# A four-layer Flamingo kernel: the 16-head attentions of layers 1 and 3 as pipelines of 16 tiles, their masks as matrix products

## The chip, the core and the metric

The kernel runs on one core of one Trainium2 chip. The metric is device time in microseconds of one execution, from launch to end. Three timed executions of the kernel before are at hand, and one execution taken by the hardware profiler. Engines are named as the profile names them: PE is TensorE (matrix products), PEld its weight loads, DVE is VectorE, ACT is ScalarE, POOL is GpSimd, SP is SyncE, which here only issues transfers.

## The reference, cut to what matters

A residual stream `x` of 2 x 1024 tokens of width 256 goes through four layers. Each layer adds a gated cross-attention to a context of 64 tokens per batch, and then a gated feed-forward block of eight experts. Only the attentions of layers 1 and 3 change:

```python
# layer 1 (layer 3 is alike, with its own weights)
qh = (q @ Wq.T + bq).reshape(B, Qlen, 16, 16).transpose(0, 2, 1, 3)     # q = layernorm(x)
kh = (k @ Wk.T + bk).reshape(B, Klen, 16, 16).transpose(0, 2, 1, 3)     # k = v = context
vh = (v @ Wv.T + bv).reshape(B, Klen, 16, 16).transpose(0, 2, 1, 3)
score = jnp.einsum('bhqd,bhkd->bhqk', qh, kh) / 4
score = jnp.where(kv_mask[:, None, None, :], score, -10000.0)           # layer 1: per key
# layer 3:  scores = jnp.where(m == 0, -1e9, scores), m per query and key
attn = jax.nn.softmax(score, axis=-1)
out = jnp.einsum('bhqk,bhkd->bhqd', attn, vh).transpose(0, 2, 1, 3).reshape(B, Qlen, 256)
x = x + tanh(g) * (out @ Wo.T + bo)
```

Layer 1 then adds `tanh(g) * sum_e (silu(h @ Wg[e]) * (h @ Wu[e])) @ Wd[e]` with `h = layernorm(x)`, over all eight experts for every token. Layer 3 routes each token to its two best experts, with a capacity of 320 places for each expert. Layer 2 has an attention of a single shared head and a routed feed-forward block.

## The kernel before

All arithmetic is float32, apart from small bfloat16 products in the routers. The 2048 tokens are 16 tiles of 128 tokens, and four tiles make a group; `xs` holds the whole residual stream in SBUF. A float32 matrix product stands in the trace as two MATMUL records.

The class `Heads` (L411) is the attention of 16 heads. `query_steps` makes the transposed queries of a group (L493, L494) and adds the output bias to `xs` on POOL (L501). Then four steps follow for each tile:

- `scores` (L503): four products of 64 rows by 256 columns (L515) put the scores of 8 heads into each of two PSUM banks. In layer 1, DVE adds the key mask (L532), finds the maxima (L547) and subtracts them (L548), and one ACT instruction takes the exponentials of all 1,024 columns (L555). In layer 3, DVE writes -1e9 over masked scores with a predicated copy (L526) and finds the negated maxima (L540); then ACT takes the exponentials of one head at a time, 16 instructions of 64 columns, with the maximum as the bias (L543).
- `turned` (L562): eight PE transposes (L571) and two ACT copies out of PSUM (L177).
- `quotients` (L579): 16 narrow products for the sums and 16 for the values (L590). In layer 1, two DVE reciprocals (L610) and one multiplication (L611) follow. In layer 3, which sets `by_log`, ACT takes a logarithm and an exponential (L602, L603) and DVE does three operations (L604 to L606).
- `output` (L614): two products with the output weights (L264), and DVE adds the result to `xs` (L621).

`norm_steps` (L230) is a layer norm of a group: statistics on DVE, the normed rows `h`, then eight transposes (L256). `h` is made by DVE (L246), or by ACT where `by_act` is set (L241).

In layer 1, `middle` (L1744) calls `first` for each group: norm, attention, the norm for the feed-forward block, and four DVE operations that prepare Strassen operands (`rhs_blocks`). Group 0 runs under pools that own all eight PSUM banks. The other three groups share two PSUM banks (`Both`) with the feed-forward block: `first(1)` is written ahead of `ffn1_group(0)`, `first(2)` behind it, and `first(3)` behind `ffn1_group(1)`. The block of a group is 672 products of 128 x 256 (L1644 and L1689; 1,344 records), in a Strassen-like scheme; POOL forms the sums of weights (L1275 to L1278). Behind each block but the last stands `last(g)`, the single-head attention of layer 2. What is written one after the other does not run so: the recording layer puts the instructions of each engine in an order of its own, as far as data and buffers allow, and so mixes the attention of a group among the products of the block before it.

In layer 3, `last_attention` (L1828) already runs the 16 tiles as one pipeline: for each step it calls `turned` of the tile before, `scores`, `quotients` of the tile before and `output` of the one before that, and puts in between them steps of the norm and queries of the group to come (`ready`) and of the norm and routing of the group that is done (`onward`).

Of the kernel before, what the change touches and what calls it, by code (L numbers as in the profile page):

```python
# [8 lines left out]
F32 = mybir.dt.float32  # L9
# [9 lines left out]
P = 128  # L19
# [11 lines left out]
EPS = 1e-5  # L31
NEG = -1.0e9

L0_W = 128
# [9 lines left out]
def kernel(ctx: ExitStack, tc: tile.TileContext, a: dict, out: bass.AP):  # L44
# [51 lines left out]
    def small_copy(src, name):  # L96
# [3 lines left out]

    ramp_b, upper_b, ones_b = (
        small_copy(t, n) for t, n in ((ramp, "ramp_b"), (upper, "upper_b"), (ones, "ones_b"))
    )
# [125 lines left out]

    def norm_steps(g, psp, hpool, hTpool=None, by_act=False):  # L230

        xg = xs[:, g * TG : (g + 1) * TG, :]
        mv, rstd = stats(xg, TG, by_act)
        yield
        h = hpool.tile([P, TG, D], F32, name="h")
        if by_act:
            off = small.tile([P, TG], F32, name="off")
            V.scalar_tensor_tensor(off, mv[:, :, 0], -1.0, rstd, ALU.mult, ALU.mult)
        for t in range(TG):
            if by_act:  # L240
                A.activation(  # L241
                    h[:, t, :], xg[:, t, :], AF.Identity,
                    bias=off[:, t : t + 1], scale=rstd[:, t : t + 1],
                )
            else:
                V.tensor_scalar(  # L246
                    h[:, t, :], xg[:, t, :], mv[:, t, 0:1], rstd[:, t : t + 1],
                    ALU.subtract, ALU.mult,
                )
            if t % 2:  # L250
                yield
        hT = (hTpool or hpool).tile([P, NC, GW], F32, name="hT")
        for c in range(NC):
            ps = psp.tile([P, GW], F32, name="ps_tr")
            for t in range(TG):
                T.transpose(ps[:, t * P : (t + 1) * P], h[:, t, c * P : (c + 1) * P], ident)  # L256
            evac(1 if by_act else c, hT[:, c, :], ps)
            yield
        return h, hT
# [151 lines left out]
    class Heads:  # L411


        def __init__(self, pre, c_bk, r_bv, r_bo, gate, key_mask, full_mask):
# [3 lines left out]
            self.live, self.qT = {}, {}  # L418

        def setup(self, psp, tag):  # L420

# [10 lines left out]
            if key_mask is not None:  # L432
                km_u = held.tile([P, B * SK // 4], I32, name="km_u")
                nc.scalar.dma_start(
                    km_u, key_mask.rearrange("b k -> (b k)").partition_broadcast(P)
                )
                km = held.tile([P, B * SK], F32, name="km")
                V.tensor_single_scalar(km, km_u.bitcast(U8), 0.0, ALU.not_equal)
                self.kbias = held.tile([P, B * SK], F32, name="kbias")
                V.tensor_scalar(self.kbias, km, -1.0, 10000.0, ALU.add, ALU.mult)  # L440
            if full_mask is not None:
                m_w = wpool.tile([P, 2048], F32, name="w")
                m_i = m_w[:, : NT * SK].rearrange("p (t k) -> p t k", k=SK).bitcast(I32)
                nc.scalar.dma_start(
                    m_i, full_mask.rearrange("b (t p) k -> p (b t) k", p=P)
                )
                self.dropm = held.tile([P, NT, SK], U8, name="dropm")
                V.tensor_single_scalar(self.dropm, m_i, 0.0, ALU.is_equal)
            for c in range(NC):
# [53 lines left out]
        def scores(self, tt, pools):  # L503
# [7 lines left out]

            pair = [pss.tile([P, 512], F32, name="ps_s") for _ in range(2)]
            for c in range(NC):
                for r in range(2):
# [4 lines left out]
                        .rearrange("p j k -> p (j k)"),  # L519
                        start=True, stop=True,  # L520
                    )
            for r in range(2):
                ps3 = pair[r].rearrange("p (j k) -> p j k", k=SK)
                ps4 = pair[r].rearrange("p (c j k) -> p c j k", c=NC, k=SK)
                if self.full_mask is not None:
                    V.copy_predicated(  # L526
                        out=ps3,
                        mask=self.dropm[:, tt, :].unsqueeze(1).to_broadcast([P, HC, SK]),
                        data=negs.unsqueeze(2).to_broadcast([P, HC, SK]),
                    )  # L530
                if self.key_mask is not None:
                    V.tensor_add(  # L532
                        ps3, ps3,
                        self.kbias[:, b * SK : (b + 1) * SK].unsqueeze(1)
                        .to_broadcast([P, HC, SK]),
                    )
                mx = two.tile([P, HC], F32, name="mx")
                if self.full_mask is not None:

# [13 lines left out]
                )  # L553
            if self.full_mask is None:
                A.activation(pr, pr, AF.Exp)  # L555
            self.live[tt] = pr

        def values(self, tt, pools):
            self.turned(tt, pools)
            self.quotients(tt, pools)  # L560

# [60 lines left out]

        def group(self, g, hT, pools):

            self.queries(g, hT, pools)
            for i in range(TG + 2):
                if i < TG:
                    self.scores(g * TG + i, pools)
                if 0 <= i - 1 < TG:
                    self.values(g * TG + i - 1, pools)  # L630
                if 0 <= i - 2:
                    self.output(g * TG + i - 2, pools)

# [1110 lines left out]
    def middle():  # L1744
        with ExitStack() as es:
            two = es.enter_context(tc.tile_pool(reuse_waits="tile", name="mi_two", bufs=2))
            hp = es.enter_context(tc.tile_pool(reuse_waits="tile", name="mi_h", bufs=1))
            hTp = es.enter_context(tc.tile_pool(reuse_waits="tile", name="mi_hT", bufs=1))
            hT1p = es.enter_context(tc.tile_pool(reuse_waits="tile", name="mi_hT1", bufs=2))
            hT1 = {}  # L1750

            def first(g, pools):
                _, hT = norm_group(g, pools["pt"], hp, hTp)
                heads1.group(g, hT, pools)
                _, hT = norm_group(g, pools["pt"], hp, hT1p)
                t = hT1p.tile([P, 4, 256], F32, name="xsum")
                hT1[g] = hT, rhs_blocks(
                    hT[:, 0, :256], hT[:, 0, 256:], hT[:, 1, :256], hT[:, 1, 256:],
                    [t[:, i] for i in range(4)],
                )  # L1760


            with ExitStack() as wide:
                pools = {"two": two}
                for n, bufs in (("pt", 2), ("ps", 4), ("py", 2)):
                    pools[n] = wide.enter_context(
                        tc.tile_pool(reuse_waits="tile", name="mw_" + n, bufs=bufs, space=PSUM)
                    )
                first(0, pools)

            py = es.enter_context(tc.tile_pool(reuse_waits="tile", name="mi_py", bufs=2, space=PSUM))
# [20 lines left out]
            pb = seed_banks(pbp)  # L1792
            first(1, pools)
            for g in range(NG):
                ffn1_group(g, hT1[g], pools, pb)
                if g + 2 < NG:
                    first(g + 2, pools)
                if g + 1 < NG:
                    run(last(g))
# [28 lines left out]
    def last_attention():  # L1828
        with ExitStack() as es:
# [15 lines left out]
            def ready(g):  # L1845
                _, hT = yield from norm_steps(g, pools["pt"], hp, hTp, by_act=True)
                yield from heads3.query_steps(g, hT, pools)

            def onward(g):
                h, hT = yield from norm_steps(g, pools["pt"], hp2, by_act=True)  # L1850
                yield from router3.group_steps(g, h, hT, pr, rp)

            run(ready(0))
            coming, gone = [], []

            def between(n):
                advance(coming)
                advance(gone, n)  # L1860

            for i in range(NT + 2):
                if i < NT and i % TG == 0:
                    advance(coming, 99)
                    if i + TG < NT:
                        coming.append(ready(i // TG + 1))
                if 0 <= i - 1 < NT:
                    heads3.turned(i - 1, pools)
                if i < NT:
                    heads3.scores(i, pools)  # L1870
                between(2)
                if 0 <= i - 1 < NT:
                    heads3.quotients(i - 1, pools)
                between(2)
                if 0 <= i - 2:
                    heads3.output(i - 2, pools)
                if i > TG and i % TG == 1:
                    gone.append(onward(i // TG - 1))
                between(1)
            advance(gone, 99)  # L1880

# [114 lines left out]
```

## Time and profile before

| what | us |
|---|---|
| timed executions | 2265.69, 2277.82, 2279.7 (median 2277.82) |
| profiled execution, its own time | 2266.35 |
| span of its trace, first to last instruction | 2264.3 |
| busy in the span: PE / DVE / ACT / POOL | 2075.5 / 1389.0 / 967.2 / 1105.6 |
| 0 to 346: layer 0 | 346, PE busy 276.3, clock 0.87 |
| 346 to 394: attention of layer 1, group 0 | 48, PE busy 35.3, clock 0.71 |
| 394 to 1682: feed-forward of layer 1, with the attention of groups 1 to 3 and three of the single-head attentions | 1288, PE busy 1272.0, clock 1.00 |
| 1682 to 1930: rest of layer 2 | 248, PE busy 205.9 |
| 1930 to 2101: attention and routing of layer 3 | 171, PE busy 141.1, clock 0.84 |
| 2101 to 2264: feed-forward of layer 3 | 163, PE busy 144.9, clock 0.93 |

The clock is the mean share of TensorE's full speed that was granted in the stretch. Matrix products are pipelined, and the ends that the trace gives them are modelled, so a busy PE is not always a PE at its peak; where it matters, starts are compared with starts.

### The profile page before, as it was taken

How to read it: one execution, taken by the hardware profiler on the slowest of the kernel's cores; microseconds unless marked ns; L12 is line 12 of the kernel's file. 1: busy time of each engine (PE TensorE's matmuls, PEld its weight loads, DVE VectorE, ACT ScalarE, POOL GpSimd, SP SyncE). 2: the span in 40 equal slices, each digit the busy share in tenths (PEclk: the TensorE clock that was granted, in tenths of full speed). 3: DMA queues.
4: the chain of work that ended last, by engine and by line, in shares of the span. 5: the costliest groups of instructions: out<-in, count | busy, mean ns of one | idle time of the engine just before them, and what ended most of it. 6: DMA issues, size and time to landing. Idle time of an engine off the chain costs nothing.

```text
span 2264.3 us, 31677 instructions
## 1 busy us (share of the span) xinstructions
PE 2075.5 (92%) x11232; PEld 1737.0 (77%) x11232; DVE 1389.0 (61%) x3199; ACT 967.2 (43%) x2200; POOL 1105.6 (49%) x1233
## 2 busy tenths in 40 slices
PE   6749997999999999999999999999985998797797
PEld 3439984788888778887788887888864998465797
DVE  5851127876655966566966556665575666576564
ACT  4414431633333533334433333333332654684454
POOL 2226643256665356665366664666631674100674
PEclk8859996999999999999999999999995999797899
DMA  3136442122222122222122222222222444111352
GB/s 101 47 127 192 127 142 85 38 75 92 86 84 75 57 84 84 88 90 70 61 88 90 84 90 78 87 91 85 90 78 72 133 128 104 47 39 57 100 143 63
DMA packets 108533, 201.05 MB, mean 89 GB/s; under 512 B 20052, under 2 KB 47960, under 8 KB 105790
## 3 DMA queue, kind: packets, MB, share of 16 engines
q1 hardware_dynamic: 83144, 162.18, 22.5%
q0 software_dynamic: 19728, 36.03, 6.2%
q8 instruction: 89, 1.46, 0.3%
q10 hardware_dynamic: 5504, 0.82, 0.2%
q14 instruction: 68, 0.56, 0.1%
HBM read 206.89 MB, written 21.91 MB: 101 GB/s over the span
## 4 chain that ended last, share of the span: by engine, by line
PE 76%; DVE 12%; DMA 4%; issue 2%; POOL 2%; ACT 2%; POOLq 0%; SPq 0%; DVEq 0%; ACTq 0%
PE ps_b L1644 14%; PE ps_a L1644 9%; PE ps_e L1644 9%; PE ps_b L1689 6%; PE ps_m L264 6%; PE ps_e L1689 4%; PE ps_a L1689 4%; PE ps_y L934 3%; PE ps_y L264 3%; PE ps_b L1485 2%; PE ps_b L1512 2%; PE ps_a L1485 2%; PE ps_e L1485 1%; PE ps_e L1512 1%; PE ps_a L1512 1%
## 5 line engine op out<-in xcount | busy, mean ns | idle before, releaser
L1644 PE MATMUL ps_b<-xsum,w 128*128 128x256 f32 x1536 | 389.6, 381 | 3.3 <-DVE c L1670 2.7
L1275 POOL TENSOR_TENSOR w<-w 128x256 f32<-128x256 f32 x220 | 162.2, 737 | 449.4 <-DMA w<-in_L_Wu_dram 182.9
L1644 PEld LDWEIGHTS ps_b<-xsum,w 128*128 128x128 f32 x1536 | 288.9, 190 | 51.4 <-issue 7.3
L1326 ACT COPY u<-ps_b 128x512 f32<-128x512 f32 (+5 forms) x242 | 119.2, 493 | 432.3 <-PE ps_b L1689 241.8
L1644 PE MATMUL ps_a<-hT,w 128*128 128x256 f32 x1024 | 266.6, 380 | 0.7 <-DVE hT L179 0.7
L1644 PEld LDWEIGHTS ps_a<-hT,w 128*128 128x128 f32 x1024 | 192.0, 190 | 29.0 <-issue 2.0
L1276 POOL TENSOR_TENSOR w<-w 128x256 f32<-128x256 f32 x220 | 190.0, 864 | 0.0
L1278 POOL TENSOR_TENSOR w<-w 128x256 f32<-128x256 f32 x220 | 181.1, 823 | 16.7
L1277 POOL TENSOR_TENSOR w<-w 128x256 f32<-128x256 f32 x220 | 188.8, 858 | 0.0
L1308 ACT COPY ps_b<-ps_a 128x512 f32<-128x512 f32 (+5 forms) x242 | 116.1, 480 | 129.7 <-DVE b L1674 75.2
L1314 ACT COPY m<-ps_e 128x512 f32<-128x512 f32 (+5 forms) x242 | 118.2, 489 | 41.0 <-PE ps_e L1689 26.7
L1644 PE MATMUL ps_e<-xsum,w 128*128 128x256 f32 x512 | 133.3, 379 | 0.0
L1644 PE MATMUL ps_e<-hT,w 128*128 128x256 f32 x512 | 132.9, 380 | 0.0
L1706 POOL TENSOR_TENSOR m<-m,accT 128x256 f32<-128x256 f32 x60 | 71.2, 1186 | 125.8 <-ACT m L1314 119.7
L1689 PE MATMUL ps_a<-b,w 128*128 128x256 f32 x512 | 132.3, 379 | 0.0
L886 POOL DMA_INDIRECT xg<-hd_L,r_idx x48 | 46.6, 971 | 175.0 <-DVE r_wsl L870 87.3
L1689 PE MATMUL ps_b<-t,w 128*128 128x256 f32 x512 | 130.9, 379 | 0.0
L1670 DVE TENSOR_TENSOR c<-ps_e,u 128x512 f32<-128x512 f32 x64 | 44.2, 691 | 136.8 <-ACT u L1326 136.8
L1671 DVE TENSOR_TENSOR b<-b,c 128x512 f32<-128x512 f32 x128 | 117.4, 917 | 3.9
L1644 PEld LDWEIGHTS ps_e<-hT,w 128*128 128x128 f32 x512 | 96.4, 190 | 14.6 <-issue 1.3
L1689 PEld LDWEIGHTS ps_b<-t,w 128*128 128x128 f32 x512 | 97.0, 190 | 13.7 <-DVE accT L1707 0.5
L1689 PEld LDWEIGHTS ps_a<-b,w 128*128 128x128 f32 x512 | 96.9, 190 | 13.9 <-issue 0.9
(423 smaller groups left out, 4550.1 us busy)
## 6 DMA issues: line engine op xcount, KB each, us to landing
w<-in_L_Wg_dram SPq DMA_DIRECT2D x64, 512.0 KB, 4.0
w<-in_L_Wu_dram SPq DMA_DIRECT2D x64, 512.0 KB, 4.0
w<-in_L_Wd_dram SPq DMA_DIRECT2D x64, 512.0 KB, 3.6
w<-in_L_W_dram SPq DMA_DIRECT2D x64, 512.0 KB, 4.3
hd_L<-h SPq DMA_DIRECT2D x8, 512.0 KB, 2.9
b<-b2d SPq DMA_DIRECT2D x23, 128.0 KB, 3.1
xs<-in_x_dram SPq DMA_DIRECT2D x4, 512.0 KB, 5.5
xd<-xs SPq DMA_DIRECT2D x4, 512.0 KB, 2.8
```

Of the source, the lines that this page charges most:

```text
L264: T.matmul(ps, lhsT=lhs(c), rhs=rhs(c), start=(c == 0), stop=(c == n - 1))
L1275: lambda: eng.tensor_add(s[0], a21, a22),
L1276: lambda: eng.tensor_sub(s[1], s[0], a11),
L1277: lambda: eng.tensor_sub(s[2], a11, a21),
L1278: lambda: eng.tensor_sub(s[3], a12, s[1]),
L1308: A.copy(self.b, self.pa)
L1314: A.copy(self.sb5, self.pe)
L1326: A.copy(u2, self.b)
L1485: T.matmul(ps[:, q * half : (q + 1) * half], lhsT=w[kind][:, q, :], rhs=x[kind], start=(first and q == 0), stop=True, skip_group_check=True,)
L1644: T.matmul(ps[:, q * 256 : (q + 1) * 256], lhsT=lhs[kind][:, q, :], rhs=xr[kind], start=(first and q == 0), stop=True, skip_group_check=True,)
L1671: V.tensor_mul(m[name], m[name], c)
L1689: T.matmul(ps, lhsT=wd[kind][:, q, :], rhs=m["rhs"][kind][:, q * 256 : (q + 1) * 256], start=(clear and q == 0), stop=True, skip_group_che ...
```

## The change

Six edits belong together.

1. **Order.** The loop of `last_attention` becomes the method `Heads.pipeline`, and layer 1 uses it too: all 16 tiles run under the eight-bank pools ahead of the first `ffn1_group`, with three `two` buffers, two query buffers and `by_log`. The normed rows and Strassen sums of all four groups are kept until their blocks (`hT1p` has four buffers instead of two).
2. **Masks.** The predicated copy of layer 3 and the addition of layer 1 go. In their place stands a bfloat16 product of 128 x 512 in front of the scores of each bank, which opens the bank's accumulation; the score products add to it. In layer 3 it is the identity times a mask of 0 and -2^60, in layer 1 a matrix of ones times a row pattern that sums to -10000 for a masked key.
3. **Maxima.** In layer 3 the second bank of each tile is done as in layer 1: DVE subtracts the maxima of 8 heads in one instruction, and ACT takes the exponentials of its 512 columns in one.
4. **Norms.** Where `halved` is set, two of the four rows of tiles of a norm go to POOL.
5. **Quotients.** In layer 1, `by_log` replaces the two reciprocals and the multiplication by the forms of layer 3.
6. **Setup.** `kbias` and `dropm` become bfloat16, with three small DVE operations more.

```diff
-    def norm_steps(g, psp, hpool, hTpool=None, by_act=False):
+    def norm_steps(g, psp, hpool, hTpool=None, by_act=False, halved=False):
...
-            if by_act:
+            if by_act and (t % 2 or not halved):
                 A.activation(
...
+            elif by_act:
+                G.tensor_scalar(
+                    h[:, t, :], xg[:, t, :], rstd[:, t : t + 1], off[:, t : t + 1],
+                    ALU.mult, ALU.add,
                 )
...
+            self.by_head = 0 if full_mask is None else 1
...
-                self.kbias = held.tile([P, B * SK], F32, name="kbias")
-                V.tensor_scalar(self.kbias, km, -1.0, 10000.0, ALU.add, ALU.mult)
+                two_rows = held.tile([P, 2], F32, name="two_rows")
+                V.tensor_scalar(two_rows[:, 0:1], partid, 0.0, 9984.0, ALU.is_equal, ALU.mult)
+                V.tensor_scalar(two_rows[:, 1:2], partid, 1.0, 16.0, ALU.is_equal, ALU.mult)
+                V.tensor_add(two_rows[:, 0:1], two_rows[:, 0:1], two_rows[:, 1:2])
+                self.kbias = held.tile([P, B * SK], BF16, name="kbias")
+                V.tensor_scalar(self.kbias, km, -1.0, two_rows[:, 0:1], ALU.add, ALU.mult)
...
-                self.dropm = held.tile([P, NT, SK], U8, name="dropm")
-                V.tensor_single_scalar(self.dropm, m_i, 0.0, ALU.is_equal)
+                self.dropm = held.tile([P, NT, SK], BF16, name="dropm")
+                V.tensor_scalar(self.dropm, m_i, 0.0, MASKED, ALU.is_equal, ALU.mult)
...
             pair = [pss.tile([P, 512], F32, name="ps_s") for _ in range(2)]
+            if self.full_mask is not None:
+                whose, drop = ident_b, self.dropm[:, tt, :]
+            else:
+                whose, drop = ones_b, self.kbias[:, b * SK : (b + 1) * SK]
+            for r in range(2):
+                T.matmul(
+                    pair[r], lhsT=whose, rhs=drop.unsqueeze(1).to_broadcast([P, HC, SK]),
+                    start=True, stop=False, skip_group_check=True,
+                )
             for c in range(NC):
                 for r in range(2):
                     T.matmul(
...
-                        start=True, stop=True,
+                        start=False, stop=True, skip_group_check=True,
                     )
...
-                if self.full_mask is not None:
-                    V.copy_predicated(
...
-                if self.key_mask is not None:
-                    V.tensor_add(
...
-                if self.full_mask is not None:
+                if r < self.by_head:
                     V.tensor_reduce(mx, ps3, AX.X, ALU.max, negate=True)
...
-            if self.full_mask is None:
+                if self.by_head:
+                    A.activation(prv[:, r], prv[:, r], AF.Exp)
+            if not self.by_head:
                 A.activation(pr, pr, AF.Exp)
...
-        def group(self, g, hT, pools):
-            self.queries(g, hT, pools)
-            for i in range(TG + 2):
...
+        def pipeline(self, pools, ready, onward):
+            run(ready(0))
+            coming, gone = [], []
+            def between(n):
+                advance(coming)
+                advance(gone, n)
+            for i in range(NT + 2):
+                if i < NT and i % TG == 0:
+                    advance(coming, 99)
+                    if i + TG < NT:
+                        coming.append(ready(i // TG + 1))
+                if 0 <= i - 1 < NT:
+                    self.turned(i - 1, pools)
+                if i < NT:
+                    self.scores(i, pools)
+                between(2)
+                if 0 <= i - 1 < NT:
+                    self.quotients(i - 1, pools)
+                between(2)
+                if 0 <= i - 2:
+                    self.output(i - 2, pools)
+                if i > TG and i % TG == 1:
+                    gone.append(onward(i // TG - 1))
+                between(1)
+            advance(gone, 99)
...
     def middle():
         with ExitStack() as es:
+            hT1p = es.enter_context(tc.tile_pool(reuse_waits="tile", name="mi_hT1", bufs=NG))
+            hT1 = {}
+            with ExitStack() as wide:
...
+                pools = {
+                    "two": wpl("two", 3), "nq": 2, "by_log": True,
+                    "pt": wpl("pt", 2, space=PSUM), "ps": wpl("ps", 4, space=PSUM),
+                    "py": wpl("py", 2, space=PSUM),
+                }
+                hp, hTp = wpl("h", 2), wpl("hT", 2)
+                def ready(g):
+                    _, hT = yield from norm_steps(g, pools["pt"], hp, hTp, by_act=True, halved=True)
+                    yield from heads1.query_steps(g, hT, pools)
+                def onward(g):
+                    _, hT = yield from norm_steps(g, pools["pt"], hp, hT1p, by_act=True, halved=True)
+                    t = hT1p.tile([P, 4, 256], F32, name="xsum")
+                    hT1[g] = hT, rhs_blocks(
...
+                heads1.pipeline(pools, ready, onward)
...
-            hT1p = es.enter_context(tc.tile_pool(reuse_waits="tile", name="mi_hT1", bufs=2))
-            def first(g, pools):
-                _, hT = norm_group(g, pools["pt"], hp, hTp)
-                heads1.group(g, hT, pools)
-                _, hT = norm_group(g, pools["pt"], hp, hT1p)
...
-                first(0, pools)
...
-            first(1, pools)
             for g in range(NG):
                 ffn1_group(g, hT1[g], pools, pb)
-                if g + 2 < NG:
-                    first(g + 2, pools)
                 if g + 1 < NG:
                     run(last(g))
```

## The prediction

> **What bounds the kernel now.** I read the page's 40 slices first, then busy times by stretch, then TensorE's timeline, then groups by shape.
>
> The slices (each 56.6 us) show PE and its granted clock:
>
> ```profile
> PE   6749997999999999999999999999985998797797
> ...
> PEclk8859996999999999999999999999995999797899
> ```
>
> Slices 8 to 30, the feed-forward block of layer 1 with three of the four attention groups in it, are PE at full clock. Slice 7 (group 0) and slices 35 to 37 (layer 3) are not. The stretches say what the block costs. Columns: stretch, length, busy time (instructions) of PE, PEld, DVE, ACT, POOL, clock, DMA:
>
> ```profile
> 480.00:715.00 235.00, 235.00 (x1090) 206.53 (x1089) 144.35 (x209) 87.13 (x167) 150.46 (x182) 1.00 0.28 87
> ```
>
> Only feed-forward products run there: 235 us / 1,089 records = 0.2158 us each. The same stretches asked for L1644 and then L1689 alone (length, PE busy, records):
>
> ```profile
> 715.00:779.00 64.00, 34.38 (x138) 1.00 0.17 52
> ...
> 715.00:779.00 64.00, 9.69 (x37) 1.00 0.17 52
> ```
>
> 175 records x 0.2158 = 37.8 us, so the other 26.2 us of these 64 are the attention of group 2. That attention is not hidden: PE is full, and every PE microsecond of it is on the path.
>
> Layer 3 (1930 to 2101) already runs the pipeline that layer 1 is to get:
>
> ```profile
> 1960.00:2050.00 90.00, 86.67 (x752) 54.82 (x754) 70.30 (x225) 77.18 (x282) 2.35 (x1) 1.00 0.09 31
> 2010.00:2030.00 20.00, 17.68 (x138) 11.07 (x138) 19.73 (x66) 17.99 (x61) 2.35 (x1) 1.00 0.14 49
> 2050.00:2076.00 26.00, 20.61 (x172) 14.95 (x163) 17.53 (x73) 13.80 (x47) 0.00 (x0) 0.74 0.06 21
> ```
>
> PE is 96% busy at full clock in its body; ACT (86%) and DVE (78%) fill up only in bursts, as where the routing stands (DVE 99%), and the last tiles run at clock 0.74. A part of PE's busy time there is no work (start, duration, line, records):
>
> ```profile
> 1970.56 0.60 PE L571 MATMUL ps_tr<-ident,pr 128*128 128x128 f32 x4
> 1971.09 0.70 PE L515 MATMUL ps_s<-kblk,qT 64*128 64x256 f32 x2
> 1971.71 0.44 PE L571 MATMUL ps_tr<-ident,pr 128*128 128x128 f32 x2
> 1972.08 0.70 PE L515 MATMUL ps_s<-kblk,qT 64*128 64x256 f32 x2
> ...
> 1980.53 1.13 PE L515 MATMUL ps_s<-kblk,qT 64*128 64x256 f32 x4
> 1981.59 0.66 PE L256 MATMUL ps_tr<-ident,h 128*128 128x128 f32 x4
> ```
>
> Two score records hold PE 0.62 us before the next instruction, four 1.06: 0.22 each and 0.19 for the change-over. Two transposes hold it 0.37 instead of 0.22: 0.15. So each piece into which a tile's scores are cut costs 0.34.
>
> **Layer 1, before.** From the first transposes of group 0 (350.92) to 394.00: 43.1 us. Then, each time the stretch less its records x 0.2158: 394 to 462, 29.6; 462 to 480, 2.2; 715 to 779, 26.2; 779 to 812, 13.8; 1045 to 1108, 26.5; 1108 to 1137, 11.5. Together 152.9. The stretch 1370 to 1405, where a block ends and layer 2's attention runs with no 16-head attention near, costs 9.8; two such parts of the above remain after the change. Share of the 16-head attention: 133.3 us.
>
> **Layer 1, after**, counted on PE.
> - Head: first transposes to the first tile's quotients took 368.17 - 350.92 = 17.2 us. Two mask additions (1.30 us, L532) leave that path; the mask products run while PE waits for the norm. 16.0. Layer 3's first two tiles stand 10 us apart where later ones stand 6.5, its clock still rising: +3.5.
> - Tiles: layer 3's quotients start at 1964.21, 1968.58, 1974.48, 1982.17 and 1990.20: 26.0 us for four tiles with one set of queries and the transposes of two norms, no routing: 6.50 a tile. Two mask products a tile come on top. No bfloat16 product of 512 columns is in the trace. Nearest from below: eight records of 128 x 120 (L1249) start 0.42 us before the next instruction, 0.44 ns a column, so 0.22 us. From above: a float32 record of 512 columns (L264) takes 0.44. I take 0.23, the same type. 6.96 a tile; 15 tiles: 104.4. They hold three sets of queries and norms instead of 3.75: -3.9. 100.5.
> - Tail: the last tile's quotients (1.0); its logarithm, exponential, three multiplications, output, statistics, norm and transposes (0.47 + 0.46 + 1.26 + 1.1 + 0.48 + 0.75 + 0.44 + 0.8 + 1.2 + 0.95 = 7.9, and eight hand-overs of 0.2 by estimate), before which, in the built order, PE, ACT and DVE hold back the block. 20 feed-forward records (4.3) stand among it. 1.0 + 9.5 - 4.3 = 6.2.
>
> 16.0 + 3.5 + 100.5 + 6.2 = 126.2: **7.1 us less**.
>
> DVE would carry per tile: maxima and subtraction 2.4, three quotient operations 1.24, residual 0.48, two statistics 1.16, norm scalars 0.45, Strassen sums 0.42: 6.1 of 6.96, under PE. ACT: exponential 1.06, copies 1.1, logarithm and exponential 0.8, queries, norms and copies 1.6: 4.5. If DVE's queue cost PE 0.5 a tile, 8 us. Of the 27 exchanges of ACT's function tables (1.28 us each) that mixing forced, 20 go; they stood beside a full PE: nothing. POOL makes 24 sums of weights (17 us) in this stage, with norm operations among them: two per norm, at no more than the 0.74 us of L1275; they end about when ACT's two do. No queue moves on SP that anyone waits for: weights are issued ahead as before, and the first six are summed before the block starts.
>
> **Layer 3.** Instructions by shape, 1940 to 2066 (busy us, mean ns | idle before):
>
> ```profile
> L543 ACT ACTIVATE pr<-ps_s,mx 128x64 f32<-128x64 f32 x256 | 57.3, 367 | 9.4 <-DVE mx L540 9.4
> ...
> L526 DVE COPY_PREDICATED_SCALAR ps_s<-dropm,negs 128x512 f32 x32 | 23.8, 750 | 19.2 <-PE ps_s L515 18.7 <-ACT rs L603 0.3
> ```
>
> - DVE loses 23.8 us and gains 16 subtractions of 0.65, 10. ACT loses 128 exponentials (0.215 each in a row, 27.5) and gains 16 of 512 columns, 0.6 by half of L555's 1.06. Neither bounds the body; it pays in PE's idle time only: 3.3 in 1960 to 2050, 5.4 in 2050 to 2076, and there 5.4 more to the low clock. Of these 14 I take 6: DVE's relief, 13 us, falls for less than half into the bursts.
> - Masks on PE: 29 of 32 products are not in the waiting at the start: +6.7.
> - Pieces: in the built order the scores stand in 22 pieces instead of 41: 19 x 0.34 = -6.5.
> - Head: the first predicated copies (1.4) go: -1.4.
>
> Sum: **7.2 us less**. Setup's small operations lie beside loads. Total -14.3, 2266.35 to 2252.
>
> [...] When ACT, DVE and POOL ran together, DVE's b<-b,c of 128 x 512, both inputs in SBUF, averaged 917 ns (L1671), and c<-ps_e,u, one from PSUM, 691 (L1670). [...]
> PE's clock was 0.71 from 346 to 394 with PE busy 73%, and 1.00 in layer 3's body at 96%. [...]
>
> **Rivals.**
> - *Better*: PE's floor. Scores 1.73, transposes 0.88, quotients 1.01, output 0.87, masks 0.46 and a quarter of queries and transposes (1.35) make 6.3 a tile; layer 1 gains 10 more, and 3.5 if the clock is up at once: total -28. For it: a lighter DVE and four score banks instead of three. Against: layer 3 at 6.5 without masks.
> - *Nothing gained*: group 0 today needs 5.8 a tile (quotients 368.17 to 385.68, three tiles) without queries and norms; with these and masks 7.6. Layer 1 then gains nothing, and if the mask products cost 0.44, layer 3 neither: 0.
> - *Slower*: the clock. Layer 1's attention leaves a stage whose feed-forward products keep PE full, and each tile waits on a chain through DVE and ACT. Layer 3's own first 27 us (1930 to 1957) have it at 0.63. If the whole stage ran so, tiles take 6.96 / 0.63 = 11.0 and 100.5 becomes 159.5: +59 - 14 = +45, 2317. With 104.4 x (1/c - 1) lost, it eats the 14.3 below a clock c of 0.88 and is slower by 1% below 0.71. Against: layer 3's body at 1.00, though beside routing.
>
> **How the numbers follow.** The profiled execution and the fastest timed one (2265.69) lie 12 to 14 us under the other two; the median of all four is 2272.1, and I count from there: 2272 - 14 = 2258. Cases: forecast 0.50, 2244 to 2271: mask products from nothing, where they lie in waits (-14), to 0.44 each (+13), idle time recovered from 0 to 14, DVE's queue +8. Better 0.25, 2234 to 2252. Nothing gained 0.13, 2266 to 2284. Slower 0.12, 2288 to 2330. The range 2234 to 2286 leaves out the last and the edges of better. One per cent, 23 us, is about what a measurement of this kernel can tell from no change. Under 2255 lie nine tenths of better (0.22) and a sixth of the forecast (0.08): faster 0.30. Over 2301 lie three quarters of slower: 0.09. The same: 0.61.
>
> **What would show it.** Layer 1: first transposes to the block's first unbroken stretch some 126 us, quotients 7 us apart, clock 1.00 after the third tile; the stretches behind the first two blocks' ends at some 10 us of other work, like the third's. Layer 3: scores in one piece, mask products near 0.22, ACT below 70%, quotients from first to last 110 us instead of 116. Wrong: tiles at 8 us or more, a DVE full for tiles on end, or a feed-forward block slower than 0.216 a record.

## The result, and the profile after

Four executions of the changed kernel took 2234.43 to 2246.75 us, median 2243.43; four of the kernel before, 2265.69 to 2279.7, median 2275.72. The ratio is 0.987, with a 95% interval of 0.984 to 0.990: faster by 1.0 to 1.6%. The prediction said 2258, in a range of 2234 to 2286, and gave the largest chance (0.61) to a change within 1%. The range held; the likeliest case did not.

The slices of the page after (each 55.8 us):

```profile
PE   5659998999999999999999999999986999797897
...
PEclk9859998999999999999999999999985999797899
```

The dip of slice 7 in PE's row is smaller (8 tenths instead of 7). The feed-forward block starts later, at about 450 us instead of 394, but no 16-head attention cuts into it any more. Cut at events that both traces show, the stages took:

| stage | before | after | difference |
|---|---|---|---|
| up to the first transposes of layer 1 | 350.9 | 341.3 | -9.6 |
| from there to the end of layer 1's feed-forward block | 1329.2 | 1318.3 | -10.9 |
| rest of layer 2, to layer 3's first transposes | 253.3 | 254.5 | +1.2 |
| layer 3, to the first tile's quotients | 20.8 | 19.4 | -1.4 |
| layer 3, to the last tile's quotients | 116.1 | 106.1 | -10.0 |
| the rest | 193.9 | 193.1 | -0.8 |

The first row is not the change's. Below is a stretch of layer 0 in the trace of before, and then in that of after (length, busy time of PE, PEld, DVE, ACT and POOL with their instructions; the third number from the end is the granted clock):

```profile
28.00:46.00 18.00, 15.32 (x32) 7.55 (x32) 5.35 (x10) 6.33 (x11) 4.89 (x3) 0.68 0.00 0
```

```profile
28.00:46.00 18.00, 13.72 (x41) 6.65 (x39) 11.27 (x27) 9.99 (x18) 6.09 (x4) 1.00 0.00 1
```

The same layer runs at a clock of 0.68 in one and 1.00 in the other. In the 14 traces of this study, layer 0 being the same in all, layer 1's first transposes start at 339.4 to 342.0 in five, which have at most 3.4 us of half clock between 17 and 49 us, and at 346.2 to 350.9 in the other nine, which have 13.6 to 20.5. One of the five (`mask_dve` below) has the setup of the kernel before, and several of the nine that of the changed kernel, so the edits do not decide it. The two profiles compared here happen to be one of each kind. What is left to the edits is some 22 us by these two traces; the ratio says 24 to 36, and part of that stays open below.

Layer 1, cut at its first transposes, the first and the last tile's quotients, and 480; then the three stretches with a single-head attention (columns as above):

```profile
341.30:359.47 18.17, 14.15 (x55) 7.86 (x55) 13.29 (x23) 7.81 (x16) 17.77 (x20) 0.80 0.08 31
359.47:450.14 90.67, 88.01 (x863) 57.91 (x862) 74.73 (x183) 56.59 (x109) 15.29 (x22) 1.00 0.02 5
450.14:480.00 29.86, 28.52 (x153) 22.32 (x153) 16.39 (x34) 16.07 (x30) 7.97 (x10) 1.00 0.15 46
715.00:780.00 65.00, 63.27 (x292) 50.68 (x291) 44.01 (x88) 24.94 (x46) 34.21 (x43) 1.00 0.26 82
1045.00:1110.00 65.00, 63.35 (x285) 50.43 (x284) 41.10 (x85) 25.04 (x45) 30.65 (x39) 0.97 0.24 77
1330.00:1405.00 75.00, 73.24 (x340) 59.74 (x339) 45.71 (x93) 30.11 (x54) 37.09 (x48) 1.00 0.25 79
```

PE is 97% busy in the body at full clock, 90.67 / 15 = 6.04 us a tile, with 4.98 of DVE and 3.77 of ACT. One tile on PE's timeline (start, duration, line, records):

```profile
376.49 0.64 PE L603 MATMUL ps_y<-pT,halves 128*32 128x128 f32 x16
376.95 0.62 PE L603 MATMUL ps_y<-pT,vblk 128*32 128x128 f32 x16
377.50 1.13 PE L273 MATMUL ps_y<-wo,oT 128*128 128x256 f32 x4
378.47 0.59 PE L536 MATMUL ps_s<-kbias,ones_b 128*128 128x512 bf16 x2
378.99 1.13 PE L542 MATMUL ps_s<-kblk,qT 64*128 64x256 f32 x6
380.05 1.09 PE L584 MATMUL ps_tr<-ident,pr 128*128 128x128 f32 x8
```

Two mask products hold PE for 0.52 us; the six score records then hold it for 1.06, where the prediction had four in 1.06. The groups of layer 3 show the same, before (1933 to 2072) and after (1914 to 2041), all 128 records in both (busy us, mean ns):

```profile
L515 PE MATMUL ps_s<-kblk,qT 64*128 64x256 f32 x128 | 38.0, 436 | 0.8 <-ACT pr L543 0.5 <-ACT qT L494 0.2
```

```profile
L558 ACT ACTIVATE pr<-ps_s,mx 128x64 f32<-128x64 f32 x128 | 28.5, 332 | 15.2 <-DVE mx L555 15.0
L542 PE MATMUL ps_s<-kblk,qT 64*128 64x256 f32 x128 | 25.7, 423 | 0.7 <-ACT qT L511 0.7
```

A record lasts as long as before (436 and 423 ns), yet 128 of them cover 25.7 us instead of 38.0. More of them run at the same time. The score products of the two banks use rows 0 to 63 and rows 64 to 127 of PE; before, layer 3 mostly issued them a bank at a time.

### The profile page after: what moved, and what is told of

It reads as the page before. It is cut to its first block, busy times and chain, and to the rows that moved or that the text cites. A ratio compares the mean times of both kernels' runs of the same rounds, so it can differ in the third digit from the quotient of the medians.

```text
span 2232.7 us, 31616 instructions
## 1 busy us (share of the span) xinstructions
PE 2057.9 (92%) x11296; PEld 1733.4 (78%) x11296; DVE 1333.7 (60%) x3059; ACT 940.6 (42%) x2124; POOL 1124.9 (50%) x1265
## 5 line engine op out<-in xcount | busy, mean ns | idle before, releaser
L1340 ACT COPY ps_b<-ps_a 128x512 f32<-128x512 f32 (+5 forms) x242 | 115.4, 477 | 120.4 <-DVE b L1706 68.7
L250 POOL TENSOR_SCALAR h<-xs,rstd,off 128x256 f32<-128x256 f32 x32 | 19.9, 632 | 220.3 <-DVE off L242 121.6
L1683 ACT ACTIVATE b<-b 128x512 f32<-128x512 f32 x128 | 80.7, 630 | 67.1 <-DVE b L1691 62.7
```

What stands on the lines that cost most here:

```text
L1340: A.copy(self.b, self.pa)
L1683: done[0] = A.activation(dst, src, AF.Silu)
```

## The experiments

Each kernel is the changed one but for its edit, and is compared with the kernel before on its chip. The stages were cut as above. "L1" is the second row of the table above, "tiles" the fifth. Kernels with the same code in a stage show its scatter: new L1 1317.3, 1318.2 and 1318.3; tiles of the changed layer 3 105.4 to 106.8 (six runs); old L1 1329.2 and 1334.2; old tiles 116.1 and 115.4. "Half" is for how many microseconds of the stage to its left PE's granted clock stood at half. Four score records of one bank took 1.06 us at full clock (in `apart`) and 2.00 at half (in the changed kernel, from 2024.96), so by estimate up to half of the "half" is time lost. It differs from run to run, and a difference between two runs can be the clock's by that much. With it taken off, the tiles of the six runs agree at 98.2 to 98.7, against 107.6 and 106.4 of the old.

| run | ratio (95% interval) | L1 | half | tiles | half |
|---|---|---|---|---|---|
| before | 1 | 1329.2 | 23.3 | 116.1 | 17.2 |
| after | 0.987 (0.984-0.990) | 1318.3 | 14.4 | 106.1 | 15.9 |
| l3_only | 0.994 (0.992-0.997) | 1334.2 | 28.2 | 106.5 | 16.5 |
| l1_only | 0.992 (0.989-0.994) | 1317.3 | 13.4 | 115.4 | 18.1 |
| unpaired | 0.988 (0.984-0.992) | 1320.1 | 12.8 | 107.9 | 18.1 |
| mask_twice | 0.989 (0.986-0.992) | 1323.6 | 12.9 | 107.0 | 6.2 |
| apart | 0.994 (0.991-0.996) | 1326.7 | 12.6 | 111.4 | 10.2 |
| mask_dve | 0.994 (0.992-0.996) | 1330.4 | 29.9 | 119.3 | 29.5 |
| head2 | 0.987 (0.985-0.989) | 1318.2 | 17.7 | 106.6 | 3.4 |
| warm | 0.986 (0.984-0.989) | 1319.1 | 12.9 | 105.4 | 13.7 |
| order_old | 0.997 (0.996-0.999) | 1337.7 | 20.5 | 105.5 | 13.7 |
| not_halved | 0.988 (0.985-0.991) | 1313.7 | 13.3 | 108.8 | 19.7 |
| reciprocal | 0.990 (0.986-0.993) | 1322.8 | 22.3 | 106.8 | 16.9 |
| key_weights | 0.984 (0.981-0.987) | 1314.7 | 21.0 | 106.7 | 16.9 |

### The layers one at a time

`l3_only` takes `middle`, `group` and layer 1's masks from the kernel before, `l1_only` layer 3's masks, exponentials and norms:

```diff
 l1_only
-            self.by_head = 0 if full_mask is None else 1
+            self.by_head = 0 if full_mask is None else 2
-            _, hT = yield from norm_steps(g, pools["pt"], hp, hTp, by_act=True, halved=True)
+            _, hT = yield from norm_steps(g, pools["pt"], hp, hTp, by_act=True)
+                if self.full_mask is not None:
+                    V.copy_predicated(
...
```

> Layer 1 exactly as before (order, masks added by DVE, reciprocals, norms), layer 3 as in the changed kernel. In the two profiles layer 3's tiles, from the first tile's quotients to the last's, fell from 116.2 to 106.2 us and its head by 1.4. If the two layers' parts add up: 11 us under the kernel before (ratio 0.995), tiles at 106 and score records in layer 3 at 26 us busy. If layer 3's gain is owed to something that layer 1 hands on (the clock, a table of ACT, buffers): ratio 1.00 and tiles near 116. The first transposes of layer 1 stood at 350.92 before and 341.30 after, with TensorE at half clock until 43 us in the one and until 17 us in the other: if that is chance, this run may show either; if an edit causes it, this run tells on which side the edit stands.

> Layer 1 as in the changed kernel, layer 3's attention exactly as before (predicated copies, all exponentials by head, norms by ACT alone). Between the first transposes of layer 1 and the end of its feed-forward block the profiles show 1329.2 us before and 1318.1 after. If the parts add up: 11 us under the kernel before (ratio 0.995), and layer 3's tiles back at 116. If the order of layer 1 brings nothing by itself: ratio 1.00.

The layers' parts are independent: each run has the new value in its own layer and the old one in the other. The ratios add up to 0.986. The first transposes stood at 339.42 and 348.8: `l3_only` shows the early kind with layer 1 as before, `l1_only` the late kind with the new layer 1.

### Score products of the two halves

`unpaired` only exchanges two loops:

```diff
-            for c in range(NC):
-                for r in range(2):
+            for r in range(2):
+                for c in range(NC):
                     T.matmul(
```

> The changed kernel with the score products of a tile written bank by bank: both products of rows 0 to 63, then both of rows 64 to 127, instead of in turn. In the built order neighbours of different halves fall from 76 to 28; the pieces do not grow (48 to 45). Theory (PE): two neighbouring products with different halves of the rows run at the same time, and layer 3 gained 12.2 us of score time with 26 more such neighbours, 0.47 us each: 48 x 0.47 = 22 us slower than the changed kernel, ratio to before 0.997, tiles of layer 3 near 116 although the masks stay on PE and the maxima with DVE. Rival (relief): the gain is DVE's and ACT's lighter load: within 4 us of the changed kernel, ratio 0.987.

It changed little (L1 +1.8, tiles +1.8), and by its expectation the theory should have fallen. The trace shows why it did not. Score records alone, a stretch of 0.1 us early and one later in a tile, first in `unpaired`, then in the kernel before where one bank's four records stand alone (length, PE busy and records, PEld, clock):

```profile
1961.30:1961.40 0.10, 0.10 (x2) 0.10 (x4) 1.00 0.00 0
1961.65:1961.75 0.10, 0.10 (x4) 0.10 (x2) 1.00 0.00 0
```

```profile
1980.60:1980.70 0.10, 0.10 (x1) 0.10 (x2) 1.00 0.00 0
1980.95:1981.05 0.10, 0.10 (x2) 0.09 (x1) 1.00 0.00 0
```

Twice as many are under way in `unpaired`, although its queue holds the four records of one half first, and all eight take 1.07 us:

```profile
1961.25 1.14 PE L542 MATMUL ps_s<-kblk,qT 64*128 64x256 f32 x8
1962.32 0.64 PE L603 MATMUL ps_y<-pT,halves 128*32 128x128 f32 x16
```

The edit had not parted them. `apart` puts a product over all rows in between:

```diff
             for r in range(2):
                 T.matmul(pair[r], lhsT=whose, rhs=drop..., start=True, stop=False, ...)
-            for c in range(NC):
-                for r in range(2):
+                for c in range(NC):
                     T.matmul(
```

> The changed kernel with each bank's mask product directly in front of that bank's score products: mask, two products of rows 0 to 63, mask, two products of rows 64 to 127. In the run with the halves written one after the other, records of both halves still started two at a time, so that run had not parted them; a product over all 128 rows between them does. Theory (halves at the same time): eight score records take 1.73 + 0.19 us instead of 0.88 + 0.19, 0.86 a tile: score records of layer 3 some 38 us busy instead of 25.7, its tiles 106 -> 116 to 120, layer 1 up to its block's end 1318 -> 1328 to 1332; 20 to 28 us slower than the changed kernel, ratio to before 0.996 to 1.000. Rival (relief of DVE and ACT): within 4 us of the changed kernel, 0.987.

```profile
1977.78 0.38 PE L536 MATMUL ps_s<-dropm,ident_b 128*128 128x512 bf16 x1
1978.09 1.13 PE L541 MATMUL ps_s<-kblk,qT 64*128 64x256 f32 x4
1979.15 0.39 PE L536 MATMUL ps_s<-dropm,ident_b 128*128 128x512 bf16 x1
1979.47 1.13 PE L541 MATMUL ps_s<-kblk,qT 64*128 64x256 f32 x4
```

Now four records take 1.06 us and the eight 2.12. Layer 3's score records cover 35.8 us instead of 25.7, layer 1's 36.7 instead of 25.8. L1 grew by 8.4, close to that; the tiles by only 5.3. PE was at half clock for 10.2 us of them instead of 15.9, which gives back up to 2.9 by estimate, so the edit cost layer 3 between 5.3 and 8.2. The theory holds, though layer 3's part came out below the 10 to 14 expected: what the records cover grows by more than the stage.

### The masks

```diff
 mask_twice
+                for again in range(2):
                     T.matmul(pair[r], lhsT=whose, rhs=drop..., start=not again, ...)
 mask_dve: no mask products, and per bank, layer 3 and layer 1
+                    V.copy_predicated(out=ps3, mask=self.dropm[:, tt, :]..., data=negs...)
+                    V.tensor_add(ps3, ps3, self.kbias[:, b * SK : (b + 1) * SK]...)
```

> The changed kernel with each mask product issued twice (the masks are added twice): 64 products of 128 x 512 more. If they lie on the path at 0.22 to 0.26 us each: 14 to 17 us slower than the changed kernel, ratio to before 0.993 to 0.995. If they run where PE waits for its chain: 0 to 4 us, ratio 0.987 to 0.989. If bfloat16 products of 512 columns really take their 0.38 us of the records: 24 us, ratio 0.998.

> The changed kernel with the masks back on DVE (the predicated copy in layer 3, the addition in layer 1) and no mask products; order, maxima, norms and quotients as in the changed kernel. In the built order layer 3's scores are then cut again: 39 pieces with 13 neighbours of different halves (22 and 38 in the changed kernel), layer 1's hardly (29 neighbours instead of 38). Theory (halves): 25 neighbours x 0.47 = 12 us lost in layer 3 and the masks' 32 products saved (0.03 to 0.23 each): tiles 111 to 117. Layer 1: DVE's 5.0 us a tile grow by 1.3 to 6.3, as long as the tile itself: block's end 0 to 6 us later. Ratio to before 0.991 to 0.996. Rival (a DVE mask costs its own time on the path): 64 x 0.7 = 45 us, ratio 1.007. Rival (masks are free on either engine and pieces do not matter): 0.987.

A second mask product costs 5.3 / 32 = 0.17 us in layer 1. In layer 3 the tiles grew by only 0.9 us, but at 6.2 us of half clock instead of 15.9; with up to 4.9 hidden there, a product costs between 0.03 and 0.18. Taking the products away lost more than that: 12.1 us in L1, and 13.2 in the tiles, which end up longer than before the change. The low clock, 15.5 and 13.6 us more of it, can account for up to 7.7 and 6.8 of these; whether the edit brought it, no run says. The body of layer 3 in `mask_dve` and in the changed kernel:

```profile
1947.70:2067.00 119.30, 111.00 (x917) 73.97 (x920) 89.34 (x284) 73.81 (x223) 7.23 (x9) 0.88 0.08 28
```

```profile
1933.50:2039.70 106.20, 102.93 (x946) 70.19 (x948) 72.86 (x252) 72.60 (x223) 6.99 (x9) 0.93 0.09 31
```

DVE carries 16.5 us more, PE idles 8.3 instead of 3.3, its clock falls from 0.93 to 0.88, and PE's busy time grows although 32 products are gone: score records cover 36.9 us again. In the built order they stand in 39 pieces, and only 13 neighbours are of different halves (22 and 38 in the changed kernel). Why the mask products keep both banks' scores together was not tested. How much of the 13.2 is DVE's load and how much the parted halves, one run does not say; `apart`, which has the parted halves alone, lost 5.3 to 8.2. Against the expectations, both bounds for L1 (0 to 6) and for the tiles (111 to 117) were too low.

### The order of layer 1

```diff
 order_old
-                heads1.pipeline(pools, ready, onward)
+            first(1, pools)
             for g in range(NG):
                 ffn1_group(g, hT1[g], pools, pb)
+                if g + 2 < NG:
+                    first(g + 2, pools)
 reciprocal
-                    "two": wpl("two", 3), "nq": 2, "by_log": True,
+                    "two": wpl("two", 3), "nq": 2,
```

> The changed kernel with layer 1's order of before (group 0 under its own pools, groups 1 to 3 among the feed-forward products, norms and quotients as before) but its masks still by products; layer 3 as in the changed kernel. With the masks on DVE the new order ended its block at 1330.4 and the old one at 1329.2 to 1334.2, with products the new one at 1317 to 1320. If order and masks are worth something only together (in the old order 24 tiles lie beside a full TensorE, where a mask product costs its time and DVE's addition cost nothing): 1332 to 1338, ratio to before 0.994 to 0.998. If the masks alone bring layer 1's gain, whatever the order: 1318 to 1322, ratio 0.987.

> The changed kernel with layer 1's quotients as before (two DVE reciprocals and a multiplication in place of ACT's logarithm and exponential and three DVE operations); order and masks as changed. DVE's load of 5.0 us a tile then changes by what two reciprocals of 128 columns take less 1.3 us, ACT's falls by 0.8. If DVE is near its limit in layer 1 (it rose from 5.0 to 6.4 a tile with the masks and the stage by 12 us): 0 to 15 us later at the block's end. If DVE does not bound it: 1318, ratio to before 0.987.

`order_old` also has layer 1's norms and quotients of before. With old order and DVE masks L1 is 1329.2 or 1334.2, with old order and products 1337.7, with new order and DVE masks 1330.4, with both 1318. By these times neither edit gains clearly by itself; with the clock's part taken off, the new order alone may gain 2 to 5 us. Among feed-forward products PE is full and DVE has time (before, from 394 to 1682: 1272.0 and 850.0 of 1288 us busy), so a mask belongs on DVE; in the pipeline it belongs on PE. The quotients by logarithm brought 4.5 us in it, of which the clock (7.9 us less of half clock) can account for up to 4.0.

### Maxima, norms, the clock

```diff
 head2
-            self.by_head = 0 if full_mask is None else 1
+            self.by_head = 0 if full_mask is None else 2
 not_halved: in both pipelines' ready and onward
-    norm_steps(..., by_act=True, halved=True)
+    norm_steps(..., by_act=True)
 warm
+            warm = pools["ps"].tile([P, 512], F32, name="ps_s")
+            for _ in range(3 if self.full_mask is None else 12):
+                T.matmul(warm, lhsT=ident, rhs=self.kblk[:, 1, 1]..., start=True, stop=True)
             run(ready(0))
```

> The changed kernel with layer 3's maxima all as before: both banks by head (256 exponentials of 64 columns on ACT). The scores then stand in 38 pieces with 23 neighbours of different halves. Theory (halves, PE is the limit): 15 x 0.47 = 7 us in layer 3's tiles, 106 -> 110 to 114; layer 1 as in the changed kernel (1318). Rival (ACT's bursts are what the edit relieves): ACT gets 13.7 us more of busy time, and the tiles go back to 116 or beyond. If the maxima change nothing: 106.

> The changed kernel with all rows of the norms in both pipelines made by ACT, none by POOL: 32 operations of 0.59 us back to ACT, 16 in each layer. Where POOL's 2.3 us addition of the output bias ran, a DVE operation of four columns took 2.1 to 2.3 us instead of 0.16. If POOL's norm rows hold DVE back in the same way: layer 1 up to 5 us less. If only ACT's time counts: 9.4 us more of ACT in a layer, which has idle time: 0 to 3 us more in each. If the split is worth what it moves: +9 in each layer, ratio to before 0.995.

> The changed kernel with float32 products that nobody reads in front of the first norm's transposes of each pipeline: 3 in layer 1, 12 in layer 3 (0.88 us each at full clock), where TensorE waits 11.5 us for the norm and then runs at half clock for 17 us. If a busy TensorE keeps its clock: layer 3 from its first transposes to the first quotients 19.4 -> 11 to 14 us and no half clock there, layer 1's first 18.2 -> 14 to 17; 5 to 10 us under the changed kernel, ratio 0.983 to 0.985. If the clock follows something else: no gain, and up to 10 us lost where the products still run when the norm is ready.

`head2`: the tiles took 106.6, half a microsecond more, and by that the split of the maxima is worth little. The clock hides the rest. Here are the changed kernel and then `head2`, from the first tile's quotients to the 14th's, and from there to the last's:

```profile
1933.51:2019.16 85.65, 84.56 (x813) 56.35 (x812) 61.46 (x213) 61.89 (x190) 5.63 (x7) 0.99 0.09 30
2019.16:2039.66 20.50, 18.32 (x133) 13.79 (x131) 11.36 (x40) 10.67 (x33) 1.36 (x2) 0.67 0.11 37
```

```profile
1937.26:2031.51 94.25, 93.22 (x823) 59.22 (x822) 61.30 (x215) 76.72 (x287) 5.61 (x7) 0.98 0.09 29
2031.51:2043.84 12.33, 11.53 (x121) 8.24 (x119) 6.90 (x23) 11.62 (x46) 1.09 (x2) 1.00 0.14 45
```

At nearly the same clock `head2` was 8.6 us behind at the 14th tile, and its score records covered 25.1 us to there instead of 17.4: in the built order they stand in 38 pieces instead of 22. It caught up in the last two tiles, at full clock instead of 0.67 and with a little less work left. By the half clock of the whole stage (3.4 us instead of 15.9, up to 6.2 lost) the edit costs 0.5 to 6.7. That fits the 4 to 8 expected of the halves. What set the clock of the last tiles, no run shows.

`not_halved`: L1 fell by 4.6 and the tiles rose by 2.7; the time as a whole does not show it. Of the 2.7, up to 1.9 are the clock's (19.7 us of half clock instead of 15.9), so a gain by the POOL rows in layer 3 is not shown. In layer 1 they cost time. DVE from the changed kernel and what POOL ran meanwhile:

```profile
361.94 0.42 DVE L618 TENSOR_TENSOR rs<-ps_y,rs 128x256 f32<-128x256 f32 x1
362.40 4.96 DVE L619 SCALAR_TENSOR_TENSOR oT<-rs,oT 128x256 f32<-128x256 f32 x1
```

```profile
362.23 0.74 POOL L1310 TENSOR_TENSOR w<-w 128x256 f32<-128x256 f32 x1
362.92 0.73 POOL L1308 TENSOR_TENSOR w<-w 128x256 f32<-128x256 f32 x1
...
365.66 0.73 POOL L1309 TENSOR_TENSOR w<-w 128x256 f32<-128x256 f32 x1
366.35 0.72 POOL L1308 TENSOR_TENSOR w<-w 128x256 f32<-128x256 f32 x1
367.15 0.79 POOL L1310 TENSOR_TENSOR w<-w 128x256 f32<-128x256 f32 x1
```

L619 takes 0.41 us in the other 15 tiles. Here it took 4.96 and ended at 367.36, right behind the first gap that POOL's row of weight sums then left (367.07 to 367.15). In `not_halved` that gap came 20 us after the first transposes instead of 26, and the same instruction took 0.67. DVE's busy time in layer 1's pipeline fell from 91.9 to 85.4 us. How much of the 4.6 is this one instruction, no run separates: counted from the first transposes, the first tile's quotients came 1.1 us earlier and the third's 2.1.

`warm` missed. In layer 3 the products kept PE busy up to the transposes:

```profile
1905.12 10.57 PE L641 MATMUL ps_s<-kblk,ident 128*128 128x512 f32 x24 [0.85 <-DVE kblk L479]
1915.71 1.41 PE L265 MATMUL ps_tr<-ident,h 128*128 128x128 f32 x8
1916.95 0.38 PE L536 MATMUL ps_s<-dropm,ident_b 128*128 128x512 bf16 x1
1920.87 2.08 PE L273 MATMUL ps_y<-hT,wq 128*128 128x512 f32 x2 [3.54 <-ACT hT L181]
```

Half clock in the head fell from 12.6 to 6.8 us, but the head stayed at 19.5: PE then waited 3.54 us for the rest of the norm. There the head hangs on the norm's chain and not on PE.

### A version that beats both

```diff
 key_weights
-                self.kbias = ...                       # layer 1, and its mask products
+                V.tensor_scalar_max(weight[:, b : b + 1], weight[:, b : b + 1], 1e-30)
+                V.tensor_scalar_mul(self.hm[b], halfmask, weight[:, b : b + 1])
+                V.tensor_scalar_mul(self.den[b], halves, weight[:, b : b + 1])
...
-                        w = halves if den else self.vblk[:, b, c * 4 + i]
+                        w = self.den.get(b, halves) if den else self.vblk[:, b, c * 4 + i]
```

> The changed kernel without layer 1's 32 mask products: masked keys, whose scores are zero already, get a weight of 1e-30 in the products for the sums and the values instead, made once in the setup (ten small DVE operations). Doubling the mask products cost layer 1 5.3 us, 0.17 each. If one costs as much as the next: layer 1's block ends at 1312 to 1315 instead of 1318.3, ratio to before 0.984 to 0.986. If the first mask product of a bank runs in a wait that remains: 1318. If what the product brings is that it claims both banks together: the pieces do not grow here (46, with 76 neighbours of different halves), so no loss from that.

0.984 (0.981 to 0.987), median 2235.41 of five; L1 1314.7, 3.6 less. It is faster than the kernel before beyond doubt; against the changed kernel the gain shows in the stage and not beyond the intervals. With `not_halved`'s norms in layer 1 alone another 4 us might go. That was not tried.

## Why the prediction was right or wrong

- **The sign, the range and the rivals.** Faster, and inside the range, but at the place of the rival "better" (-28) and not of the forecast (-14). That rival's mechanism, PE's floor with every score record at 0.22, was not what happened: eight records took 1.06 us, 0.13 each. It also put all that it added to the forecast in layer 1, 20.6 us there and 7.2 in layer 3; measured were 10.9 and 11.4. So the place is luck. The rival by the clock did not come: 1.00 in layer 1's body.
- **"Tiles: 6.50 a tile" is the step that failed.** Layer 1's 15 tiles were built on layer 3's of before, in which the scores cost 38.0 / 16 = 2.37 us each because the two halves were issued apart. In layer 1's pipeline they cost 25.8 / 16 = 1.61. 15 x 0.76 = 11.4 us stand against a gap of 11.2 between the 120.0 predicted from the first transposes to the last quotients (16.0 + 3.5 + 100.5) and the 108.8 measured (18.2 + 90.7). What of it was on the path, `apart` shows: parting the halves again cost L1 8.4. The two mask products were right: 0.52 shown, 0.46 taken.
- **The rest of layer 1.** Tail: 29.86 - 101 x 0.2158 = 8.1, predicted 6.2. The single-head stretches were taken as unchanged at 9.8 each; less their records they are 11.1, 12.6 and 10.7, 5.0 more in all (the second has a dip of the clock). So the pipeline with its tail came out 9.3 us better than summed, the rest of the block about 5.5 worse, and the block gained 10.9 where 7.1 was summed.
- **"Each piece costs 0.34"** priced the cuts of layer 3's scores by the change-over alone: -6.5. A cut also parts the halves. Score records fell by 12.3 us, and `apart` shows that much of such a difference is time: 10.1 us more of them made the tiles 5.3 to 8.2 longer.
- **"Masks on PE: +6.7"** in layer 3 was too much: 29 products at the 0.03 to 0.18 of a second one are 0.9 to 5.2. **"DVE's relief"** was put at 6 us of idle time recovered, for masks and maxima together; PE's idle time in the tiles fell from 6.9 to 3.3. Most of the gain is the scores' instead. Taken back alone, the maxima cost 0.5 to 6.7 and the masks 6.4 to 13.2, with score records at 31.5 and 36.9 us: layer 3's gain needs both edits. **"Head: -1.4"** agrees by luck: with the same layer 3 the head took 17.4 to 20.8 us, before the change 20.6 and 20.8.
- **Setup's small operations**, taken as nothing: no run shows a cost. The 9.6 us seen there are the clock's.
- **The rivals' arithmetic** has a slip that moves no bound: 104.4 x (1/c - 1) makes the kernel slower by 1% below a clock of 0.74, not 0.71.
- **Norm rows on POOL** were given no cost on DVE in the sum. Measured against `not_halved`, they cost layer 1's pipeline 6.5 us of DVE's busy time (91.9 against 85.4) and L1 4.6. The weight sums on POOL then reached further into the first quotients, where L619 took its 4.96 us.
- **Open.** By stages the edits bring 22 us, by the ratio 24 to 36. Old L1 was 1334.2 in `l3_only` and 1329.2 in the profile of before; with the mean of the two it is 24, and the 4.9 us more of half clock in the first account for up to 2.5 of their difference. The rest would need traces of more executions of the kernel before, which were not taken.

## What to carry to other kernels

Before a stage's time per step is taken over to another stage, ask what in it is due to the order in which that stage happened to be built; here a third of PE's score time was (38.0 against 25.7 us). Products that use different rows of PE were worth keeping next to each other here: the product over all rows that `apart` puts between them doubled their time, from 1.07 to 2.12 us for eight records. Two kernels should be compared by stage with the clock of each stage beside it: half a microsecond in `head2` hid several. A step moved off a full engine is worth what it costs there only in the stage where that engine is the bound: the same mask products lost 3.5 to 8.5 us in the old order of layer 1 and won 12 in the new, of which up to 7.7 may be the clock's.

## What the runs showed of the hardware

- Products over rows 0 to 63 and rows 64 to 127 ran at the same time even when the queue held both products of one half first (`unpaired`): eight records in 1.07 us, against 2.12 with a full-row product in between (`apart`), a factor of 2.0.
- One DVE instruction with two inputs in SBUF took 4.96 us, where it took 0.41 in the other 15 tiles, while seven instructions of POOL ran in a row without a gap. It ended at 367.36, right behind the first gap that they left (367.07 to 367.15). That is one event; what held the instruction, no run separates.
- Layer 0, the same instructions in 14 traces, ended 4 to 12 us later in the nine that ran at half clock for 13.6 us or more between 17 and 49 us than in the five with 3.4 or less. What decides which kind an execution is, no run shows.
